# A two-layer graph attention kernel: the first layer's row gathers wait for other matmuls, one wait for each of a pair

## The chip, the cores and the metric

The kernel runs on one core of one Trainium2 chip. A time is the device time of one execution in microseconds. The engines are TensorE (PE in the profile, PEld for its weight loads), VectorE (DVE), ScalarE (ACT), GpSimd (POOL) and SyncE (SP); POOL also issues the indirect transfers (gathers) with which this text deals.

## The reference

Eight graphs of 2048 nodes share one 0/1 adjacency matrix; every node has 64 features. A first attention layer has four heads, a second one has one. Both take the scores from the same projected features on both sides, mask them by the adjacency matrix (with the diagonal set), apply a softmax over the neighbours and average the neighbours' features.

```python
def _gat_layer(h, mask, b):
    scores = jnp.einsum('...nd,...md->...nm', h, h)
    scores = jnp.where(mask, scores, NEG)
    attn = jax.nn.softmax(scores, axis=-1)
    return jnp.einsum('...nm,...md->...nd', attn, h) + b

mask = graph + jnp.eye(N, dtype=graph.dtype) > 0
h = jnp.einsum('bnc,hdc->bhnd', x, Wh)
out_h = _gat_layer(h, mask[None, None], bh[None, :, None, :])
cat = jnp.transpose(out_h, (0, 2, 1, 3)).reshape(B, N, H * D)
z = jax.nn.leaky_relu(cat, negative_slope=0.2)
h2 = jnp.einsum('bnk,dk->bnd', z, Wo)
out2 = _gat_layer(h2, mask[None], bo)
z2 = jax.nn.leaky_relu(out2, negative_slope=0.2)
# layer norm of z2, times gamma, plus beta; then the layer norm of x + that
```

The matrix is sparse: the inputs draw an edge with a probability that falls with the node numbers, 0.4% on the average, and the first nodes have far more neighbours than the rest.

## The kernel before

The first 56 nodes ("hubs") are attended against all 2048 nodes. The other 1992 nodes are cut into 166 sets of 12 (`NS`, `SET`). For each set, VectorE picks the 128 nodes that are neighbours of any of its members and writes their numbers into one column of `index`. The kernel then never forms the full attention matrix: for each set it gathers the 128 rows of features of those nodes from a table in device memory, and attends the 12 members against them under a mask.

A row holds all eight batches, 4 x 130 float32 numbers or 2,080 bytes, so one gather brings 128 rows or 266 KB into one buffer of the pool `rowp`, which has 10 buffers. One gather is one `indirect_dma_start` on POOL's queue (function `gather`, L790 to L793).

The program is written out by hand: every engine runs its instructions in the order in which the program names them, and a framework adds the semaphore waits that the data and the reuse of buffers require. There are three stages: hubs, picks and adjacency loads (to about 150 us in the profile), the first layer's loop (to about 600 us), the second layer.

The first layer's loop (L1017 to L1083) handles two sets at a time, a group; there are 83 groups (`NG`), and step `i` works on several of them at once, each at another stage of its life:

- `scores(i + 1)` (L814): 64 small matmuls; VectorE adds the mask (`weigh`, L826), ScalarE exponentiates (`lift`, L833).
- `project(i - 1)` (L525, matmuls at L531): the head outputs of the group before go through the head weights; ScalarE adds the bias (`leaky`, L518).
- `values(i)` (L837, 32 matmuls at L846): the weighted sums of the gathered rows. It is the last reader of the two row buffers of group `i`. VectorE divides by the sums (`invert`, L848 to L854).
- the gathers of group `i + LOOK`, `LOOK` being 5: both are named right after `values(i)`, and reuse the two buffers that it has just read.
- `own_rows` every second step (POOL, L800), `add_beta` every second step of a later part (POOL, L928), one adjacency load with its conversion in the first nine steps (`more(1)`, POOL at L680 and L687), `keep_own` (POOL, L886), all on POOL's queue in this order.
- `second_maps`, `second_rows`, `columns` (L880, L890, L806): the later life of earlier groups, and the query side of a later one.
- `turn` of the first set of group `i + 3` (L512), `turn_values(i)` (L863, four transposes of the divided sums), `turn` of the second set of group `i + 3` (L512). `turn` is the first reader of a gathered buffer.

So a group gathered in step g - 5 is first read by `turn` near the end of step g - 3, and last by `values` in step g. Ahead of the loop, three groups are gathered; steps -2 and -1 gather groups 3 and 4 into the remaining four of the ten buffers.

The gather before:

```python
def gather(table, s, layer, new):
    t = rows[layer, s] = new(f"g{layer}_{s}")
    nc.gpsimd.indirect_dma_start(out=t.rearrange("n q c -> n (q c)"), out_offset=None, in_=table,
                                 in_offset=bass.IndirectOffsetOnAxis(ap=index[:, s:s + 1], axis=0))
```

Of the kernel before, what the change touches and what calls it, by code (L numbers as in the profile page):

```python
# [359 lines left out]
def fast_kernel(ctx: ExitStack, tc: tile.TileContext, x, adj, Wh, bh, Wo, bo, gamma, beta, out, flag):  # L360


    nc = tc.nc
    B, N, C = x.shape
    H, D, _ = Wh.shape
# [9 lines left out]
    NG = NS // 2  # L375
    M = SET * H
    GM = 2 * Q * SET
# [21 lines left out]
    def half(k):  # L399
        return slice(k * 64, (k + 1) * 64)  # L400
# [10 lines left out]
    ident = const.tile([P, P], F32, name="ident")  # L411
# [4 lines left out]
    whT = early.tile([P, H * D], F32, name="whT")  # L416
# [8 lines left out]
    table1 = dram.tile([N, ROW], F32, name="table1")  # L425
# [9 lines left out]
    index = const.tile([P, NS], I32, name="index")  # L435
# [78 lines left out]
    def leaky(cat, n, name):  # L514

        z = work.tile([P, HP, 2, n], F32, tag="z", name=name, bufs=3)
        for hp in range(HP):
            nc.scalar.activation(z[:, hp], cat[:, :, hp * n:(hp + 1) * n], AF.Identity, bias=bhp[:, hp:hp + 1], scale=1.0)  # L518
        return z

    def leak(z):
        f = z.rearrange("p q s n -> p (q s n)")
        nc.vector.scalar_tensor_tensor(f, f, SLOPE, f, OP.mult, OP.max)

    def project(ot, cat, n):  # L525

        for hp in range(HP):
            for s in range(2):
                for j in range(2):
                    h = 2 * hp + j  # L530
                    nc.tensor.matmul(cat[half(j), s, hp * n:(hp + 1) * n], whT[half(s), h * D:(h + 1) * D],  # L531
                                     ot[half(s), h, :], start=True, stop=True)


    hubm = early.tile([HUB, N], BF16, tag="a", name="hubm", bufs=5)
# [86 lines left out]
    def hub_later(t, new):  # L622

        n = 2 * HUB
        osb = hub_osb[t]

        def turn_back():
            pt = new(f"oth{t}", "T")
            for v in range(2):
                for k in range(2):  # L630
                    nc.tensor.transpose(pt[:, 0, (2 * v + k) * P:(2 * v + k + 1) * P], osb[:, v, k, :], ident)
            ot = held["oth", t] = work.tile([P, H, n], F32, tag="ot", name=f"otbh{t}")
            nc.scalar.copy(ot.rearrange("c h (w n) -> c h w n", w=8),
                           pt[:, 0, :].rearrange("c (w n) -> c w n", w=8)[:, :, :HV].rearrange("c w (n h) -> c h w n", h=H))

        def through_heads():
            cat = new(f"cath{t}", "C")
            project(held.pop(("oth", t)), cat, n)
            z = held["zh", t] = leaky(cat, n, f"zh{t}")
            leak(z)  # L640

        def to_table():
            z = held.pop(("zh", t))
            ph = new(f"hh{t}", "S")
            for p in range(2):
                for hp in range(HP):

                    v = z[:, hp, p, :].rearrange("d (v k m) -> d k v m", v=2, k=2)
                    nc.tensor.matmul(ph[half(p), 0, :n], woT[:, hp, :], v, start=(hp == 0), stop=(hp == HP - 1))
            nc.vector.tensor_copy(ownh[:, t, :], ph[:, 0, :n])  # L650
            nc.tensor.transpose(ph[:n, 1, :P], ownh[:, t, :], ident)
            r = rowts[t]
            nc.vector.tensor_tensor(r[:n, 1:1 + P], ph[:n, 1, :P], bob[:n].rearrange("n p d -> n (p d)"), OP.add)
            dst = table2[:HUB, :].rearrange("n (q c) -> q n c", q=Q)
            for k in range(2):
                nc.sync.dma_start(out=dst[2 * t + k], in_=r[k * HUB:(k + 1) * HUB])

        return [turn_back, through_heads, to_table]
# [128 lines left out]
    rows = {}  # L787
    held = {}

    def gather(table, s, layer, new):  # L790
        t = rows[layer, s] = new(f"g{layer}_{s}")
        nc.gpsimd.indirect_dma_start(out=t.rearrange("n q c -> n (q c)"), out_offset=None, in_=table,  # L792
                                     in_offset=bass.IndirectOffsetOnAxis(ap=index[:, s:s + 1], axis=0))  # L793

    def own_rows(m):

# [17 lines left out]
    def scores(g, sp):  # L814
        xt = held.pop(("T", 1, g)).rearrange("c j (q n) -> c j q n", q=Q)
        y = held["y", g // 2][:, g % 2 * GM:(g % 2 + 1) * GM, :].rearrange("p n h -> p (n h)")
        for j in range(2):
            for q in range(Q):
                for p in range(2):
                    for r in range(2):  # L820
                        nc.tensor.matmul(sp[half(r), p, (q * 2 + j) * M:(q * 2 + j + 1) * M], xt[half(p), j, q, half(r)],  # L821
                                         y[half(p), (j * Q + q) * M:(j * Q + q + 1) * M], start=True, stop=True)
# [33 lines left out]
    def turned(op):  # L856
        return op.rearrange("a j (k c) -> a (j k) c", k=2)[:, :, 2 * (D + 2):2 * (D + 2) + 112]

    def turn_values(g, op):

        osb = held.pop(("o", g))
        for w in range(4):
            nc.tensor.transpose(turned(op)[:, w, :], osb[:112, w].rearrange("a s c -> a (s c)"), ident[:112, :112])  # L863

    def keep_values(g, op):

# [85 lines left out]
    def turns():  # L952
        return bool(picks) and getattr(picks[0], "turns", False)
# [35 lines left out]
    hub_values(*pend)  # L989
    while picks:  # L990
        picks.pop(0)()
    LOOK = 5
    for g in range(LOOK - 2):
        for j in range(2):
            gather(table1, 2 * g + j, 1, rows_tile)
    own_rows(0)
# [10 lines left out]
    def one(name, tag):  # L1007
        return psum1.tile([P, 2, 512], F32, tag=tag, name=name)
# [5 lines left out]
    ready, done = FIRST, 2 * FIRST  # L1014
    todo3 = [(10, 0), (14, 1)]
    slow = hub_later(0, one) + hub_later(1, one)
    for i in range(-4, NG + 3):  # L1017
        if 0 <= i + 1 < NG:
            sp = one(f"s{i + 1}", "S")
            scores(i + 1, sp)  # L1020
            weigh(i + 1, sp)
        if i >= 1 and slow and len(slow) % 3:
            slow.pop(0)()
        cat = one(f"cat{i}", "C")
        if 0 <= i - 1 < NG:
            project(held.pop(("ot", i - 1)), cat, GM)
            held["z", i - 1] = leaky(cat, GM, f"z{i - 1}")
        if 0 <= i + 2 < NG:
            t = held["T", 1, i + 2] = work.tile([P, 2, 512], F32, tag="xTg", name=f"xTg{i + 2}", bufs=3)
            nc.scalar.copy(t, held.pop(("tp", i + 2)))  # L1030
        if 0 <= i + 1 < NG:
            lift(i + 1)
        if 0 <= i < NG:
            op = one(f"o{i}", "O")
            values(i, op)
            invert(i, op)
        if 0 <= i + LOOK < NG and i > -3:
            for j in range(2):
                gather(table1, 2 * (i + LOOK) + j, 1, rows_tile)
        if i + 6 < NG and i % 2 == 0 and i >= -2:  # L1040
            own_rows((i + 6) // 2)
        if 0 <= (i - 30) // 2 <= NV:
            (add_beta if i % 2 else load_own)((i - 30) // 2)
        if 0 <= i - 1 < NG:
            leak(held["z", i - 1])
        if i >= 0:
            if turns():
                some(1)
            if slow and len(slow) % 3 == 0:
                slow.pop(0)()  # L1050
            more(1)
            if todo3 and i == todo3[0][0]:
                make_keys(2, todo3.pop(0)[1], late_two)
            if not picks:
                ready = done
            if not picks and not todo3 and done < NS:
                picks = pick(2)
                done = NS
            assert i + 1 + LOOK >= NG or 2 * (i + 1 + LOOK) + 1 < ready

        if 0 <= i - 2 < NG:
            second_maps(i - 2, cat[:, 0, 384:384 + GM])
        if 0 <= i - 3 < NG:
            second_rows(i - 3, cat[:GM, 1, 384:512])
        if 0 <= i + 4 < NG + NG % 2:
            columns(i + 4, cat)
        if 0 <= i - 2 < NG:
            keep_own(i - 2, cat[:, 0, 384:384 + GM])
        if 0 <= i - 3 < NG:
            keep_rows(i - 3, cat[:GM, 1, 384:512])  # L1070
        for _ in range((2 if i < 22 or i % 2 else 1) if i >= 0 else 0):
            if not turns():
                some(1)
        if 0 <= i + 4 < NG + NG % 2:
            keep_columns(i + 4, cat)
        if 0 <= i + 3 < NG:
            tp = held["tp", i + 3] = one(f"t{i + 3}", "T")
            turn(tp[:, 0, :], rows[1, 2 * (i + 3)])
        if 0 <= i < NG:
            turn_values(i, op)  # L1080
            keep_values(i, op)
        if 0 <= i + 3 < NG:
            turn(tp[:, 1, :], rows[1, 2 * (i + 3) + 1])  # L1083
# [267 lines left out]
    for u in range(-4, NU + 7):  # L1351
        if 0 <= u + 2 < NU:
            scores2(u + 2)
        if 0 <= u < NU:
            a = u % 2
            if a == 0:
                op = bank2(f"o2_{u}", "O")
# [18 lines left out]
        if 0 <= u + 1 < NU:  # L1376
            turn_scores(u + 1)
            a = (u + 1) % 2
# [55 lines left out]
```

## Time and profile before

| What | Value |
|---|---|
| time, median of 3 runs | 1042.88 us (1037.15 to 1049.1) |
| the profiled execution: own time | 880.76 us |
| its span, first to last instruction | 878.9 us |
| mean granted TensorE clock in it | 0.951 |
| TensorE busy (matmuls) | 753.0 us, 86% of the span |
| VectorE, ScalarE, GpSimd busy | 610.1, 514.4, 469.2 us |
| gathers (both layers) | 332, in all 334.9 us busy on POOL, 1009 ns mean |
| gathers' bytes | 88.55 of 145.22 MB moved |

A line of the list of groups or of the timeline gives the source line, the engine, the operation, and the tiles as written<-read, with the count. Times in brackets are an engine's idle time before the instruction and what ended it. The busy time of a gather on POOL is that of its issue; the landing of its data shows only in semaphore events and in what waits for them. The profiled execution was shorter than the timed ones by 162 us; the page shows the profiled one alone.

### The profile page before, as it was taken

How to read it: one execution, taken by the hardware profiler on the slowest of the kernel's cores; microseconds unless marked ns; L12 is line 12 of the kernel's file. 1: busy time of each engine (PE TensorE's matmuls, PEld its weight loads, DVE VectorE, ACT ScalarE, POOL GpSimd, SP SyncE). 2: the span in 40 equal slices, each digit the busy share in tenths (PEclk: the TensorE clock that was granted, in tenths of full speed). 3: DMA queues.
4: the chain of work that ended last, by engine and by line, in shares of the span. 5: the costliest groups of instructions: out<-in, count | busy, mean ns of one | idle time of the engine just before them, and what ended most of it. 6: DMA issues, size and time to landing. Idle time of an engine off the chain costs nothing.

```text
span 878.9 us, 42066 instructions
## 1 busy us (share of the span) xinstructions
PE 753.0 (86%) x18437; PEld 661.2 (75%) x18437; DVE 610.1 (69%) x1369; ACT 514.4 (59%) x961; POOL 469.2 (53%) x612
## 2 busy tenths in 40 slices
PE   1896777889999999999999999992999999998730
PEld 1664456778788999988999999971899999988720
DVE  3356983568888788877555555553258999998994
ACT  2342333556556667666766667651678888886821
POOL 5654141457444555655666666503777777777300
PEclk9998998999999999999999999995999999999965
DMA  8787451355434445655566665514888888888611
GB/s 167 238 218 213 129 146 48 83 142 160 109 100 118 112 125 159 162 169 153 160 168 173 160 166 162 134 28 114 246 266 253 275 275 267 266 252 242 172 46 35
DMA packets 81794, 145.22 MB, mean 165 GB/s; under 512 B 30146, under 2 KB 46466, under 8 KB 81602
## 3 DMA queue, kind: packets, MB, share of 16 engines
q0 software_dynamic: 26720, 88.55, 36.4%
q1 hardware_dynamic: 37842, 49.65, 18.7%
q10 hardware_dynamic: 17040, 4.25, 2.6%
q8 instruction: 147, 2.41, 1.1%
q14 instruction: 45, 0.37, 0.1%
HBM read 123.91 MB, written 18.48 MB: 162 GB/s over the span
## 4 chain that ended last, share of the span: by engine, by line
PE 63%; DVE 15%; DMA 7%; ACT 5%; issue 4%; SPq 3%; POOL 2%; DVEq 0%; ACTq 0%; POOLq 0%
PE t L512 11%; PE s L821 10%; PE o L846 10%; PE cat L806 6%; PE o L863 4%; PE cat L531 4%; PE cat L880 3%; PE s L1133 3%; PE o L1165 3%; PE cat L890 2%; DMA raw<-in_adj_dram 2%; SPq L1248 2%; PE sh L1277 2%; PE e L1144 2%; DMA g<-table,index 1%
## 5 line engine op out<-in xcount | busy, mean ns | idle before, releaser
L792 POOL DMA_INDIRECT g<-table,index x332 | 334.9, 1009 | 236.1 <-PE o L846 140.2
L512 PE MATMUL t<-ident,g 128*128 128x128 f32 x1328 | 182.3, 276 | 15.6 <-DMA g<-table,index 12.7
L512 PEld LDWEIGHTS t<-ident,g 128*128 128x128 f32 x1328 | 154.8, 142 | 20.0 <-issue 14.0
L826 DVE TENSOR_TENSOR e<-s,mask 128x768 f32<-128x768 f32 x83 | 79.4, 956 | 87.4 <-PE s L821 85.4
L518 ACT ACTIVATE z<-cat,bhp 128x192 f32<-128x192 f32 x166 | 60.8, 418 | 85.0 <-PE cat L531 85.0
L846 PE MATMUL o<-g,e 128*64 128x65 f32 x2656 | 97.5, 227 | 0.0
L821 PEld LDWEIGHTS s<-y,xTg 64*64 64x64 f32 x5312 | 85.2, 134 | 13.9 <-issue 13.7
L821 PE MATMUL s<-y,xTg 64*64 64x48 f32 x5312 | 95.5, 220 | 0.0
L846 PEld LDWEIGHTS o<-g,e 128*64 128x64 f32 x2656 | 85.8, 140 | 9.8
L1320 ACT COPY xTg<-t 128x1024 f32<-128x1024 f32 x83 | 80.3, 1017 | 18.1 <-PE t L512 17.3
L1030 ACT COPY xTg<-t 128x1024 f32<-128x1024 f32 x83 | 84.0, 1012 | 2.0 <-PE t L512 2.0
L833 ACT ACTIVATE e<-e,shifts 128x768 f32<-128x768 f32 x83 | 79.2, 955 | 2.1 <-DVE e L826 1.7
L812 ACT COPY y<-cat 128x384 f32<-128x384 f32 (+1 forms) x80 | 40.7, 508 | 64.0 <-PE o L863 40.1
L597 ACT ACTIVATE e<-e,shifts 128x896 f32<-128x896 f32 x32 | 33.4, 1042 | 73.0 <-DVE e L594 52.1
L680 POOL TENSOR_SCALAR a<-raw 120x1024 bf16<-120x1024 int32 (+1 forms) x34 | 38.2, 1125 | 65.1 <-DMA raw<-in_adj_dram 38.4
L806 PE MATMUL cat<-xo,gram 128*128 128x192 f32 (+1 forms) x320 | 65.6, 328 | 0.0
L853 DVE RECIPROCAL rall<-o 64x8 f32<-64x8 f32 x166 | 34.0, 205 | 42.0 <-PE o L846 40.7
L854 DVE TENSOR_TENSOR osb<-o,rall 128x512 f32<-128x512 f32 x83 | 57.4, 692 | 2.9
L1165 PE MATMUL o<-g,es 128*32 128x65 f32 x2656 | 49.1, 226 | 5.9 <-DVE y_s L1188 4.5
L806 PEld LDWEIGHTS cat<-xo,gram 128*128 128x128 f32 x320 | 53.7, 203 | 0.3 <-issue 0.2
L1165 PEld LDWEIGHTS o<-g,es 128*32 128x32 f32 x2656 | 46.1, 113 | 7.0 <-issue 4.9
L1133 PE MATMUL s<-xTg,bd 128*32 128x128 f32 x1328 | 45.4, 277 | 6.2 <-ACT bd L1124 3.5
(177 smaller groups left out, 1369.3 us busy)
## 6 DMA issues: line engine op xcount, KB each, us to landing
raw<-in_adj_dram SPq DMA_DIRECT2D x32, 480.0 KB
table<-xb SPq DMA_DIRECT2D x22, 256.0 KB
xr_s<-table SPq DMA_DIRECT2D x21, 256.0 KB
g<-table,index POOLq DMA_INDIRECT x332
table<-x SPq DMA_DIRECT2D x16, 260.0 KB
x<-in_x_dram ACTq DMA_DIRECT2D x32, 128.0 KB
table<-rowt SPq DMA_DIRECT2D x166, 24.4 KB
xb<-in_x_dram SPq DMA_DIRECT2D x164, 24.0 KB
```

The costliest lines, as they stand in the source:

```text
L512: nc.tensor.transpose(tp[:, q * P:(q + 1) * P], rows[:, q, 1:1 + P], ident)
L518: nc.scalar.activation(z[:, hp], cat[:, :, hp * n:(hp + 1) * n], AF.Identity, bias=bhp[:, hp:hp + 1], scale=1.0)
L792: nc.gpsimd.indirect_dma_start(out=t.rearrange("n q c -> n (q c)"), out_offset=None, in_=table, in_offset=bass.IndirectOffsetOnAxis(ap=ind ...
L806: nc.tensor.matmul(cat[:, k, 2 * GM:2 * GM + n], gram[:, g % 2 * 2 + k, :], held["x", g // 2][:, :n], start=True, stop=True)
L821: nc.tensor.matmul(sp[half(r), p, (q * 2 + j) * M:(q * 2 + j + 1) * M], xt[half(p), j, q, half(r)], y[half(p), (j * Q + q) * M:(j * Q + q ...
L826: nc.vector.tensor_tensor(e[:, :16 * M].rearrange("p (a q n) -> p a q n", a=2, q=Q), sp[:, :, :8 * M].rearrange("p a (q n) -> p a q n", q= ...
L833: nc.scalar.activation(e[:, :16 * M], e[:, :16 * M], AF.Exp, bias=shifts[:, 0:1], scale=1.0)
L846: nc.tensor.matmul(op[half(p), j, o0:o0 + K1], e[:, c0:c0 + 64], rw[j][:, q, sums(p)], start=True, stop=True)
L1030: nc.scalar.copy(t, held.pop(("tp", i + 2)))
L1133: nc.tensor.matmul(sp[q * 32:(q + 1) * 32, k, :], bd[u % 3][:, k, q, :], xt[:, s % 2, q, :], start=True, stop=True, tile_position=(0, q * 32))
L1165: nc.tensor.matmul(op[t * 32:(t + 1) * 32, f, k * W2 + p:k * W2 + p + K1], e[:, 2 * q + p, k, :], rw[:, q, sums(p)], start=(a == 0 and k = ...
L1320: nc.scalar.copy(t, tp)
```

## The change

A gather may now be given an instruction that it has to wait for, besides what its buffer requires. `project` and `turn_values` return their last matmul, and the loop hands these on. The first set's gather of a group is named at the very beginning of a step and waits for the turned values of the step before; the second one is named where both were named, and waits for the projection of its own step. The distance falls from five groups to four; steps -2 and -1 gather groups 3 and 4 as before, step 0 gathers none, and from step 1 on step `i` gathers group `i + 4`.

```diff
@@ project
-                    nc.tensor.matmul(cat[half(j), s, hp * n:(hp + 1) * n], whT[half(s), h * D:(h + 1) * D],
-                                     ot[half(s), h, :], start=True, stop=True)
+                    at = nc.tensor.matmul(cat[half(j), s, hp * n:(hp + 1) * n], whT[half(s), h * D:(h + 1) * D],
+                                          ot[half(s), h, :], start=True, stop=True)
+        return at
@@ gather
-    def gather(table, s, layer, new):
+    def gather(table, s, layer, new, behind=None):
         t = rows[layer, s] = new(f"g{layer}_{s}")
-        nc.gpsimd.indirect_dma_start(out=t.rearrange("n q c -> n (q c)"), out_offset=None, in_=table,
-                                     in_offset=bass.IndirectOffsetOnAxis(ap=index[:, s:s + 1], axis=0))
+        g = nc.gpsimd.indirect_dma_start(out=t.rearrange("n q c -> n (q c)"), out_offset=None, in_=table,
+                                         in_offset=bass.IndirectOffsetOnAxis(ap=index[:, s:s + 1], axis=0))
+        if behind is not None:
+            tc.add_manual_dep(g.ins, behind.ins.name, mybir.DependencyInfo(mybir.DependencyClass.Sync, mybir.DependencyReason.DATA),
+                              reason="the gather's turn")
@@ turn_values
         for w in range(4):
-            nc.tensor.transpose(turned(op)[:, w, :], osb[:112, w].rearrange("a s c -> a (s c)"), ident[:112, :112])
+            at = nc.tensor.transpose(turned(op)[:, w, :], osb[:112, w].rearrange("a s c -> a (s c)"), ident[:112, :112])
+        return at
@@ ahead of the loop
-    LOOK = 5
-    for g in range(LOOK - 2):
+    LOOK = 4
+    for g in range(3):
@@ the loop
+    turned_at = projected_at = None
     for i in range(-4, NG + 3):
+        coming = i + LOOK if i > 0 else i + LOOK + 1 if -2 <= i < 0 else NG
+        if coming < NG:
+            gather(table1, 2 * coming, 1, rows_tile, turned_at)
...
-            project(held.pop(("ot", i - 1)), cat, GM)
+            projected_at = project(held.pop(("ot", i - 1)), cat, GM)
...
-        if 0 <= i + LOOK < NG and i > -3:
-            for j in range(2):
-                gather(table1, 2 * (i + LOOK) + j, 1, rows_tile)
+        if coming < NG:
+            gather(table1, 2 * coming + 1, 1, rows_tile, projected_at)
...
-            turn_values(i, op)
+            turned_at = turn_values(i, op)
```

## The prediction

> **What bounds the kernel now.** I first read the busy shares and the windows, to find which engine sets the length of the first layer's loop.
>
> ```profile
> span 878.9 us, 42066 instructions
> PE 753.0 (86%) x18437; PEld 661.2 (75%) x18437; DVE 610.1 (69%) x1369; ACT 514.4 (59%) x961; POOL 469.2 (53%) x612
> ...
> 400.00:500.00 100.00, 99.62 (x2718) 90.90 (x2711) 60.42 (x145) 67.39 (x138) 61.93 (x80) 1.00 0.60 164
> 225.00:590.00 365.00, 357.90 (x9742) 324.76 (x9742) 255.87 (x655) 241.17 (x497) 197.76 (x262) 1.00 0.52 140
> ```
>
> The columns of the last two lines are stretch, length, and busy time of PE, PEld, DVE, ACT and POOL, then the granted clock, DMA share and GB/s. From 400 to 500 us TensorE is busy for 99.62 of 100 us at full clock, from 225 to 590 us for 357.9 of 365: it sets the step. The list of waits must then say whether any of its few pauses is for a gather.
>
> ```profile
> PE t L512 <- DMA g<-table,index: 12.7, 4, 10.7
> POOL g L792 <- PE o L846: 127.6, 70, 5.2
> POOL a L680 <- DMA raw<-in_adj_dram: 5.4, 2, 2.9
> ```
>
> The first line is of the whole run. All four of its waits lie in the second layer's start near 611 us; TensorE's waits from 150 to 590 us hold none for a gather. The other two, of 180 to 590 us, say who releases the gathers today: the 32 matmuls of `values` (L846), because the buffer to be filled is the one that they have just read. Now one step on the timeline, POOL first (start, length, instruction, and in brackets the idle time before it), then TensorE.
>
> ```profile
> 402.22 0.98 POOL L792 DMA_INDIRECT g<-table,index  x1 [0.88 <-PE o L846]
> 403.51 0.96 POOL L792 DMA_INDIRECT g<-table,index  x1 [0.30 <-PE cat L806]
> 404.47 0.66 POOL L800 COPY xo<-xT 128x192 f32<-128x192 f32 x1
> 405.10 0.25 POOL L886 COPY own<-own 128x96 f32<-128x96 f32 x1
> 408.03 0.97 POOL L792 DMA_INDIRECT g<-table,index  x1 [2.68 <-PE o L846]
> ```
>
> ```profile
> 404.06 0.60 PE L863 MATMUL o<-ident,osb 112*128 112x112 f32 x4 [0.34 <-DVE osb L854]
> ...
> 406.22 0.56 PE L531 MATMUL cat<-otb,whT 64*64 64x96 f32 x16
> ...
> 413.93 0.60 PE L512 MATMUL t<-ident,g 128*128 128x128 f32 x4
> ...
> 414.75 0.60 PE L512 MATMUL t<-ident,g 128*128 128x128 f32 x4
> ```
>
> The reader should see a step of about 5.0 us (402.22 to 408.03 held one pause; 413.93 to 418.9 is the usual gap between turns), the two new releasers (turned values at 404.06, projection at 406.22), and the turns at 413.93 and 414.75 that read the two gathers issued at 402.22 and 403.51.
>
> **What the Trainium skill says.** "DMA: Bandwidth & Descriptors", section "Anatomy of one DMA — SWDGE (gpsimd) path", prices such a DMA at about 2.0 us plus bytes over 436 GB/s; one gather is 128 rows of 2,080 B, 266 KB, so an estimate of 2.6 us. The trace agrees: from the semaphore events, the last count of a gather of the first layer arrives 2.3 us at least, 2.75 us in the median after its issue instruction ends, 4.5 us at most from the fortieth gather on, and up to 7.1 us while adjacency loads run beside it. "Perfetto Trace Analysis", section "DMA Instruction — SWDGE (GPSIMD)", says that the profile's interval of such an instruction ends with the descriptors, not with the data; the same numbers show it (0.97 us against 2.75 more). "TensorE: Matmul & The Clock Gate" lists, in its opening table, GpSimd's queue as strict first-in first-out; below, a gather is seen to stand behind a conversion that waits for its load. The same page, Part 1, says that TensorE idle for some 3.4 us falls to half clock; here the granted clock is 0.70 in the gap from 590 to 630 us.
>
> **The change part by part.**
> *Removed:* the release by `values` and one group of distance. A gather for group g used to be issued in step g-5 behind `values`; now the first is issued behind the turned values of step g-5, the second behind the projection in step g-4. No matmul, copy or DMA is added, and the order on TensorE, VectorE, ScalarE and SyncE is the same; on POOL the pair moves past the own-rows copy, the beta addition, the adjacency conversion and the own copy of one step. Instructions: 332 gathers x 0.97 us before and after, nothing saved.
>
> *Steady steps.* For the group turned at 413.93 and 414.75: the first gather may go at 404.66 by its wait, but the own copy stands before it on POOL until 405.35, so 405.4 + 0.97 + 2.75 = 409.1, 4.8 us early (today 402.22 + 0.98 + 2.75 = 405.95, 8.0 early). The second: projection done at 406.78, issue to 407.9, landed at 410.6, 4.1 early (today 7.5). So about 3.2 us of distance is given away and 4 us is left: nothing on the path. What hides the wait is TensorE's own step; without that cover each late microsecond would be paid every second step, since the turn of group g delays the releases of group g+2. The new waits hold only POOL behind them: the own-rows copy (used two steps later), the beta addition, the conversion, the own copy. All these sit *earlier* after the change, as both releases come before `values`. Replaying POOL's new order with each gather's own landing time, the median spare falls from 7.1 to 4.2 us and the worst after group 14 is 1.6 us, so still nothing.
>
> *Early steps.* Here adjacency loads are still running:
>
> ```profile
> 189.36 1.00 POOL L792 DMA_INDIRECT g<-table,index  x1 [5.19 <-PE o L846]
> ...
> 194.83 1.15 POOL L680 TENSOR_SCALAR a<-raw 120x1024 bf16<-120x1024 int32 x1 [2.50 <-DMA raw<-in_adj_dram]
> ...
> 206.87 1.13 POOL L680 TENSOR_SCALAR a<-raw 120x1024 bf16<-120x1024 int32 x1 [2.95 <-DMA raw<-in_adj_dram]
> ```
>
> Today group 9 is gathered at 189.36, ahead of the conversion that waits for its load. Afterwards it stands behind it: POOL is free at 197.1, issue 197.6 to 198.6, landing 4.8 later as this gather had it, 203.4; its turn is at 201.92: 1.5 us late. The next conversions do the same to groups 10 and 11: the second of 10 is late by 0.5, the two of 11 by 1.5 and 0.4, on top of the slip before. Sum 3.9 us. Bounds: 0, if TensorE had to stand for VectorE's picks there anyway (it is busy 23.87 of 25 us from 200 to 225, so hardly); 4.9, with one microsecond more per landing. I take 3.9. A gain below zero is excluded in the steady part beyond TensorE's idle time: 390 us from 200 to 590 less 381.8 busy leaves 8 us, 0.8% at the very most.
>
> *Sum.* The profiled execution took 880.76 us (span 878.9 and 1.9 around it); plus 3.9 gives 884.7, +0.4%. The median of the timed runs is 1042.88, 162 us or 18% above the profiled one, and nothing in the page says where that lies. Were TensorE's 753 us to run at a clock of 0.78 in place of 0.951, it would be explained (753 x 0.951/0.78 = 918, an estimate); then steps are longer and the spare larger (replayed at steps 1.2 times as long: 2.6 us lost). On the timed runs: 1042.9 + 4 = 1047.
>
> **The rivals.**
> *A, slower:* the unexplained 162 us is late gathers. Place: the turns (L512) of steady steps. It decides from a landing of about 7 us after the issue's end (2.75 + the 4 spare); with 4.5 us more than in the profile, the second gathers (spare 3.8 in the median of the replay) are 0.7 late each and, paid every second step, 78/2 x 0.7 = 27, with the early 4 it is 31: 1074. If gathers bind the kernel before as well, the whole given-away distance, 39 x 2.9 = 113 us, is the end of that road. For it: the gap, and that the loop's DMA share is 0.52 to 0.6. Against: the profile shows no landing that long in steady steps.
> *B, faster:* issuing at the step's edge keeps descriptor writing away from VectorE's reciprocal and product (L853, L854), which TensorE's turn of values awaits, or spreads the two transfers. Against: gathers take 942 ns at least and 974 in the median, so nothing holds them up, and TensorE waits 1.7 us in all for L854. Only something outside the profile could pay; a tenth of the 162 us gives 1027.
> *C, no effect:* the early slip is absorbed and the release order is not binding: 1043.
>
> **How the numbers follow.** Forecast (early slip alone, 1043 to 1052) 0.36, C 0.16, A 0.34, B 0.14. About 1% is what a measurement of this kernel can tell from no change. Forecast and C lie within 1% but for noise (0.46 of 0.52, the rest going to slower); A is slower save for its mildest end (0.02), so slower 0.38, same 0.48, faster 0.14. The range reaches from half-way into B (1030) to a little past A's value (1080); B's better half and A's far end are left out.
>
> **What would show it.** In the profile after: POOL's gathers released by L863 and L531 (their shifted lines) in place of L846; no TensorE wait for a gather from 225 to 590 us; one to four such waits from 198 to 220 us summing to about 4 us; the window 400 to 500 still over 99% busy. I am wrong if the turns wait for gathers throughout (A), or if the timed runs fall by more than 10 us without the profile's steps becoming shorter (B).

## The result, and the profile after

The changed kernel takes 1128.23 us (median of 4, 1125.46 to 1137.13); the kernel before, measured beside it, 1044.79. The ratio is 1.082 [1.073, 1.091]: 83 us slower. The prediction said 1047, with a range to 1080.

The runs fall into two groups by the chip that they ran on: on some chips ("A" below, three of the later sets of runs) the kernel before takes some 880 us, on others ("B", two sets) some 1040. What makes a chip A or B is not known. The profile of before that stands above has the time of A, while the timed runs, and the profile after, have that of B. So the profile after is set against another profile of the kernel before, taken on B in a later run (span 1043.4 us).

The busy shares, the score matmuls' group and the window from 400 to 500 us of after (the group's columns are busy time and mean ns, then the idle time before it and what ended most of that; the window's are those of the prediction):

```profile
span 1127.5 us, 42067 instructions
PE 872.9 (77%) x18437; PEld 711.7 (63%) x18437; DVE 610.6 (54%) x1369; ACT 514.0 (46%) x961; POOL 460.3 (41%) x612
...
L825 PE MATMUL s<-y,xTg 64*64 64x48 f32 x5312 | 134.6, 223 | 32.6 <-issue 29.9
...
400.00:500.00 100.00, 89.01 (x2112) 74.96 (x2112) 57.65 (x157) 52.26 (x108) 47.62 (x62) 1.00 0.46 128
```

The kernel before on B, the same window:

```profile
400.00:500.00 100.00, 97.25 (x2497) 87.05 (x2497) 58.20 (x142) 63.34 (x127) 57.38 (x75) 1.00 0.55 152
```

At full granted clock (1.00) TensorE gets through 2112 matmuls in 100 us instead of 2497, and it does not only pause more: 42.1 ns of busy time stand for one matmul against 38.9. The waits say what it doesn't wait for. TensorE's of after from 150 to 800 us:

```profile
PE s L825 <- issue: 29.9, 70, 0.7
PE o L867 <- DVE osb L858: 18.8, 71, 1.5
...
PE t L512 <- DMA g<-table,index: 12.5, 2, 10.5
```

POOL's from 200 to 800 us:

```profile
POOL g L793 <- PE cat L531: 83.0, 57, 2.9
POOL g L793 <- PE t L512: 29.8, 65, 1.2
```

The second gather is released by the projection (L531), as the change says. The first goes after the turned values, but what holds it last is POOL's own copy ahead of it (L891, which waits for VectorE): the gather starts 0.44 us after that copy's end in all steady steps, on A as on B, so the turn (L512) that the list names is only the signal that came last. The only two waits of TensorE for a gather stand at the start of the second layer (one of 10.5 us, as before); not one lies in the first layer's loop. Instead there are 29.9 us of pauses in the middle of the scores (L825) for which the profile shows no releaser at all ("issue"). One step of after shows where they lie (times as start and length):

```profile
416.25 1.15 PE L850 MATMUL o<-g,e 128*64 128x65 f32 x32
...
416.59 0.96 POOL L793 DMA_INDIRECT g<-table,index  x1 [1.45 <-PE cat L531]
...
417.23 0.50 PE L885 MATMUL cat<-z,woT 128*64 128x96 f32 x8
...
418.07 0.42 DVE L857 RECIPROCAL rall<-o 64x8 f32<-64x8 f32 x2 [1.10 <-PE o L850]
...
419.27 0.60 PE L867 MATMUL o<-ident,osb 112*128 112x112 f32 x4 [0.21 <-DVE osb L858]
...
419.92 0.27 POOL L891 COPY own<-own 128x96 f32<-128x96 f32 x1 [1.84 <-DVE own L890]
...
420.25 1.29 PE L825 MATMUL s<-y,xTg 64*64 64x48 f32 x48
...
420.62 0.97 POOL L793 DMA_INDIRECT g<-table,index  x1 [0.43 <-PE t L512]
...
421.95 0.46 PE L825 MATMUL s<-y,xTg 64*64 64x48 f32 x14 [0.41 <-issue]
...
422.25 0.54 PE L531 MATMUL cat<-otb,whT 64*64 64x96 f32 x15
...
422.71 1.15 PE L850 MATMUL o<-g,e 128*64 128x65 f32 x32
```

And one step of before on B:

```profile
421.27 0.95 POOL L792 DMA_INDIRECT g<-table,index  x1 [0.30 <-issue]
...
422.45 1.35 PE L821 MATMUL s<-y,xTg 64*64 64x48 f32 x64
...
423.60 0.56 PE L531 MATMUL cat<-otb,whT 64*64 64x96 f32 x16
424.10 1.15 PE L846 MATMUL o<-g,e 128*64 128x65 f32 x32
...
425.08 0.50 PE L880 MATMUL cat<-z,woT 128*64 128x96 f32 x8
...
425.30 0.42 DVE L853 RECIPROCAL rall<-o 64x8 f32<-64x8 f32 x2 [0.50 <-PE o L846]
...
425.42 0.97 POOL L792 DMA_INDIRECT g<-table,index  x1 [2.42 <-PE o L846]
```

Before, from the first score to the projection it is 423.60 - 422.45 = 1.15 us, and the reciprocal starts 1.20 us after `values` (425.30 - 424.10). After, a gather is issued *on top of* the scores, at 420.62 to 421.59: they take 422.25 - 420.25 = 2.00 us and stand still for a part of it. The other gather is issued on top of `values`, at 416.59 to 417.55: the reciprocal comes 418.07 - 416.25 = 1.82 us after it.

The two delays are not of one kind. The scores' matmuls start late. Those of `values` do not: the block takes 1.15 us in both kernels, and the next one (L885, before L880) starts 0.98 us after it in both. What is late is the semaphore event that tells of the last `values` matmul. It comes 0.64 us after that matmul's recorded end (median; late in 67 of 68 steps), in the step of before 0.02 us. Since the ends of matmuls are modelled in these profiles, it is open whether the work or only its signal was late.

As medians of the steps 20 to 70 (distances between the starts of the blocks, in us):

| | step | scores to projection | projection to `values` | `values` to reciprocal | turn to turned values | the two issues start, after the scores' start |
|---|---|---|---|---|---|---|
| before on A | 5.00 | 0.97 | 0.46 | 1.20 | 0.44 | 2.75 and 4.02 |
| before on B | 5.35 | 1.28 | 0.49 | 1.20 | 0.44 | 3.09 and 4.38 |
| after on B | 6.45 | 1.92 | 0.54 | 1.82 | 0.80 | 0.37 and 2.80 |

From the second row to the third the path on TensorE gains 0.64 at the scores, 0.05 at the projection and 0.36 where the turned values wait for the later reciprocal, 1.05 in all, and the step 1.10. Times 78 changed steps that is 86 us; the first layer's last `values` ends at 708.3 us after and at 623.4 before, 84.9 later, while what follows is as long as before (419 and 420 us). So nearly the whole loss lies at these places; that the issues are its cause is still a theory: **while POOL issues a gather, and shortly after, TensorE's blocks of many small matmuls are slowed or stopped or their end is told late, and its blocks of a few large ones keep their pace.** Before, both issues fell on the columns and turns (L806, L512), where the step shows no loss; the change moved them onto the scores and `values`. The rival is the prediction's: the gathers come later, by a group less of distance, and something waits for them.

### The profile page after: what moved, and what is told of

Same layout as the page of the kernel before. It is cut to its first block, busy times and chain, and to the rows that moved or that the text cites. A ratio compares the mean times of both kernels' runs of the same rounds, so it can differ in the third digit from the quotient of the medians.

```text
span 1127.5 us, 42067 instructions
## 1 busy us (share of the span) xinstructions
PE 872.9 (77%) x18437; PEld 711.7 (63%) x18437; DVE 610.6 (54%) x1369; ACT 514.0 (46%) x961; POOL 460.3 (41%) x612
## 3 DMA queue, kind: packets, MB, share of 16 engines
q0 software_dynamic: 26720, 88.55, 29.5%
## 4 chain that ended last, share of the span: by engine, by line
PE 63%; DVE 16%; issue 10%; ACT 4%; DMA 3%; POOL 1%; SPq 0%; another core or an unknown queue 0%; ACTq 0%; DVEq 0%; POOLq 0%
PE t L512 14%; PE o L850 11%; PE s L825 11%; DVE osb L858 4%; PE s L1141 4%; PE o L867 4%; PE o L1173 3%; PE cat L531 3%; DVE rall L857 3%; PE e L1152 2%; PE sh L1285 2%; ACT xTg L1328 2%; PE oh L1307 1%; PE sh L591 1%; DVE e L595 1%
## 5 line engine op out<-in xcount | busy, mean ns | idle before, releaser
L793 POOL DMA_INDIRECT g<-table,index x332 | 324.2, 976 | 357.6 <-PE o L1173 126.2
L512 PE MATMUL t<-ident,g 128*128 128x128 f32 x1328 | 204.3, 285 | 26.3 <-DMA g<-table,index 12.6
L512 PEld LDWEIGHTS t<-ident,g 128*128 128x128 f32 x1328 | 161.6, 147 | 47.1 <-issue 38.6
L825 PE MATMUL s<-y,xTg 64*64 64x48 f32 x5312 | 134.6, 223 | 32.6 <-issue 29.9
L825 PEld LDWEIGHTS s<-y,xTg 64*64 64x64 f32 x5312 | 107.8, 134 | 63.3 <-issue 62.1
L1160 DVE TENSOR_TENSOR es<-e,linked 128x384 f32<-128x384 f32 (+1 forms) x42 | 23.1, 550 | 138.2 <-PE t L512 109.7
L1141 PE MATMUL s<-xTg,bd 128*32 128x128 f32 x1328 | 62.9, 302 | 29.4 <-issue 19.7
L891 POOL COPY own<-own 128x96 f32<-128x96 f32 x83 | 22.8, 275 | 148.8 <-DVE own L890 148.8
L1141 PEld LDWEIGHTS s<-xTg,bd 128*32 128x32 f32 x1328 | 41.8, 120 | 46.4 <-issue 36.7
L867 PE MATMUL o<-ident,osb 112*128 112x112 f32 x332 | 49.9, 273 | 18.8 <-DVE osb L858 18.8
```

The lines of the kernel that those rows point to most:

```text
L512: nc.tensor.transpose(tp[:, q * P:(q + 1) * P], rows[:, q, 1:1 + P], ident)
L793: g = nc.gpsimd.indirect_dma_start(out=t.rearrange("n q c -> n (q c)"), out_offset=None, in_=table, in_offset=bass.IndirectOffsetOnAxis(ap ...
L867: at = nc.tensor.transpose(turned(op)[:, w, :], osb[:112, w].rearrange("a s c -> a (s c)"), ident[:112, :112])
L1141: nc.tensor.matmul(sp[q * 32:(q + 1) * 32, k, :], bd[u % 3][:, k, q, :], xt[:, s % 2, q, :], start=True, stop=True, tile_position=(0, q * 32))
```

## The experiments

### Distance against place (kind A)

The first set takes the change apart. *Distance alone*: both gathers behind `values` as before, but for one group later, so four groups ahead as in the changed kernel.

```diff
         if coming < NG:
-            gather(table1, 2 * coming, 1, rows_tile, turned_at)
...
-            gather(table1, 2 * coming + 1, 1, rows_tile, projected_at)
+            for j in range(2):
+                gather(table1, 2 * coming + j, 1, rows_tile, values_at)
```

> Both gathers of a group stay where they were, behind the values matmuls, but one group later (for group i+4 in step i, the first waiting for this step's values): only the shorter distance of the change is kept, by one whole step. S: issues fall on the same work as before, so 1043 (1035 to 1052). Theory R (late gathers, the prediction's rival A): the distance is shorter than in the changed kernel, so at least its 1128.

*First release alone*: the changed kernel with its second added wait left out; with four groups of distance the buffer has long been free, so the second gather follows the first at once.

```diff
-            gather(table1, 2 * coming + 1, 1, rows_tile, projected_at)
+            gather(table1, 2 * coming + 1, 1, rows_tile)
```

> The changed kernel without the second wait: the first gather is released by the turned values, the second follows as soon as its buffer and POOL are free. S: both issues now fall on the scores and the projection, 0.65 us each, so about as slow as the changed kernel, 1100 to 1135. R: the second gather comes earlier than in the changed kernel, so faster than it, 1043 to 1090.

*Second release alone*: the first gather of a group in its old place behind `values`, five groups ahead; only the second behind the projection.

```diff
+        if 0 < i and i + 4 < NG:
+            gather(table1, 2 * (i + 4) + 1, 1, rows_tile, projected_at)
+        if 0 <= i + 5 < NG and i > -3:
+            gather(table1, 2 * (i + 5), 1, rows_tile)
```

> The first gather of a group stays behind the values matmuls of step g-5, the second waits for the projection of step g-4 as in the change. S: one stall in a step, on the values matmuls, so about half of the loss, 1075 to 1095. R: the second gather is the later one and binds, so the whole loss, about 1128.

And the kernel before once more:

> The kernel before, once more with a profile. Theory S (issue on TensorE: while POOL writes a gather's descriptors, TensorE stands still for about 0.65 us, and the scores (L821) and values (L846) matmuls cannot hide it): about 1043 us; a first-layer step of 5.0 to 5.4 us, since both issues fall on the columns and turns, and a second layer as long as in the changed kernel (about 420 us from the last values matmul of the first layer to the end, against 287 in the shown profile), with stalls at its gather issues. Theory P (phase of POOL and VectorE: the pair's new place makes the own copy, the beta addition and VectorE's leaky product collide): also 1043, but with no stall of TensorE at a gather's issue. Rival theory C (granted clock): 1043 with a mean clock under 0.85.

Measured beside a before of 881.85 us: distance alone 886.92, ratio 1.004 [1.001, 1.007]; first release alone 932.85, 1.056 [1.051, 1.061]; second release alone 894.34, 1.013 [1.009, 1.018]; before again 884.02. The expected times for this set were numbers of kind B and missed in the absolute; in ratios, distance alone costs next to nothing, while the kernel that moves both issues forward in the step, at the same distance, loses most. TensorE's waits of distance alone from 200 to 600 us:

```profile
PE t L512 <- DMA g<-table,index: 2.6, 4, 0.9
```

Four late gathers, 2.6 us: this is the early slip that the prediction had priced at 3.9, and half of the 5.1 us that this kernel loses. A step of first release alone:

```profile
406.17 1.51 PE L825 MATMUL s<-y,xTg 64*64 64x48 f32 x64
406.18 0.98 POOL L793 DMA_INDIRECT g<-table,index  x1 [0.44 <-PE o L867]
...
407.46 0.96 POOL L793 DMA_INDIRECT g<-table,index  x1 [0.30 <-issue]
...
407.70 0.81 PE L531 MATMUL cat<-otb,whT 64*64 64x96 f32 x16
...
408.44 1.15 PE L850 MATMUL o<-g,e 128*64 128x65 f32 x32
```

The first issue lies on the scores, the second on the projection: in the medians the first take 1.18 us instead of 0.97, and the projection's distance to `values` is 0.87 instead of 0.46. That is 0.62 us of the 0.78 by which the median step grows; times 78 it is some 48 of the 51 us lost. On A the rival of late gathers falls, and the theory of the place stands; on B the changed kernel's loop, without one wait for a gather, says the same.

### The change again, its first half, and POOL busy without a gather (kind B)

> The kernel before, with a profile on the same chip as the three that follow. Theory S (a gather's issue slows TensorE's scores and projection, its values hardly or not, its larger matmuls not at all): on a chip like that of the last runs 882 with a step of 5.0 us; on a chip like that of the first times 1043, a step of 5.0 to 5.4 us and stalls in the second layer.

> The changed kernel on the chip of these runs. S: its first gather is issued on the scores, its second on the values, so if the kernel before takes 882 here, it lands between the two halves measured, 905 to 935, with the scores stretched from 0.93 to some 1.3 us; if the kernel before takes 1043 here, 1128. Theory R (late gathers): the turns wait for gathers by several tens of us in all.

*First moved alone*: the first gather behind the turned values, the second behind `values`.

```diff
-            gather(table1, 2 * coming + 1, 1, rows_tile, projected_at)
+            gather(table1, 2 * coming + 1, 1, rows_tile, values_at)
```

> The first gather of a group is released by the turned values as in the change, the second by the values matmuls of step g-4, so it stays on the columns and turns. S: one issue a step on the scores, the second free: where the kernel before takes 882, 900 to 925 (0.25 to 0.5 us in each of 78 steps); where it takes 1043, 1080 to 1110. R: the second gather is the later one and has less distance than in the change, so at least as slow as the changed kernel.

*Before with memsets*: the kernel before with four fills of a tile of 128 x 128 on POOL, named where the changed kernel has its first gather, and behind the same instruction.

```diff
+        if 0 < i and i + 4 < NG:
+            m = nc.gpsimd.memset(idle, 0.0)
+            for _ in range(3):
+                nc.gpsimd.memset(idle, 0.0)
+            tc.add_manual_dep(m.ins, turned_at.ins.name, ...
```

> The kernel before, with four memsets of a 128x128 tile added on POOL in each step from 1 to 78, released by the turned values, where the change issues its first gather: POOL is as busy there as with a gather's issue (about 1 us), but nothing is transferred. S: it is the issue of a gather that TensorE feels, not work on POOL, so within 1% of the kernel before. Rival P (POOL's occupation at that point delays what stands behind it): a good part of the loss of the change.

Measured beside a before of 1045.88 us: before again 1045.3; the change again 1123.73, 1.076 [1.069, 1.084]; first moved alone 1094.52, 1.047 [1.039, 1.055]; with memsets 1047.84, 1.004 [1.001, 1.006]. In first moved alone the second issue starts 3.72 us after the scores and touches nothing (the reciprocal is back at 1.20 after `values`), the first starts at 0.17 and stretches the scores to 1.78; the step is 5.86, 0.51 over before, times 78 some 40 of the 49 us. So each half of the change has a price of its own: about 49 us for the first issue on the scores, some 30 more when the second falls on `values`. The window of the kernel with memsets from 400 to 500 us:

```profile
400.00:500.00 100.00, 97.15 (x2477) 86.83 (x2472) 59.16 (x145) 63.47 (x128) 71.48 (x145) 1.00 0.55 150
```

POOL is busy for 71.48 us instead of 57.38, TensorE for 97.15 as against 97.25. The fills do not all fall on the scores, as other work of POOL stands before them: of 51 steps (20 to 70) they lie on the scores for over 0.4 us in 21, where the scores take 1.35 us, and not at all in 20, where they take 1.27. So POOL at work beside the scores costs them some 0.08 us at that overlap, and a gather's issue 0.5 to 0.64 us more than before.

### The issue against its transfer, and no gathers at all

*No gathers in the loop*: the changed kernel, where from the sixth group on no gather is made, the first ten buffers are read over and over, the mask is left open and the flag that asks for a general kernel is held at zero, so the attention of those groups is not that of their sets.

```diff
-            gather(table1, 2 * coming, 1, rows_tile, turned_at)
+            gather(table1, 2 * coming, 1, rows_tile, turned_at) if coming < 5 else again(2 * coming)
...
-            gather(table1, 2 * coming + 1, 1, rows_tile, projected_at)
+            gather(table1, 2 * coming + 1, 1, rows_tile, projected_at) if coming < 5 else again(2 * coming + 1)
```

> The changed kernel without the first layer's gathers from group 5 on: the ten row buffers of groups 0 to 4 are used again and again, under an open mask, and the flag that asks for the general kernel is held at zero (156 transfers and the masking of real neighbours are left out; every other instruction stays). Theory S (a gather's issue stops TensorE): the loop's step falls to 5.0 us, so where the kernel before takes 1045, 1015 to 1035; where it takes 882, 870 to 885. Theory P (POOL's order and VectorE): the step stays at 5.4 us or more.

*Quarter gathers*: the changed kernel, where each of those gathers brings 128 rows of a quarter of the length (520 B): as many descriptors, a quarter of the bytes. Its rows, mask and flag are not those of the reference either.

```diff
-        g = nc.gpsimd.indirect_dma_start(out=t.rearrange("n q c -> n (q c)"), out_offset=None, in_=table,
+        g = nc.gpsimd.indirect_dma_start(out=t[:, 0, :] if part else t.rearrange("n q c -> n (q c)"), out_offset=None,
+                                         in_=table.rearrange("n (q c) -> (n q) c", q=Q) if part else table,
```

> The changed kernel with its first-layer gathers from group 5 on a quarter as long: 128 runs of 520 bytes in place of 2,080, into the buffers of groups 0 to 4, with open mask and the flag held at zero as in the run without gathers. S in its form 'the writing of the descriptors stops TensorE': as many descriptors, so as slow as the changed kernel (within 1.5%; 1110 to 1135, or its time on the other kind of chip). S in its form 'the transfer of the data does': a quarter of the bytes, so most of the loss is gone.

*Both behind the projection*: both gathers of a group behind the projection of their step.

```diff
-            gather(table1, 2 * coming, 1, rows_tile, turned_at)
...
+            for j in range(2):
+                gather(table1, 2 * coming + j, 1, rows_tile, projected_at)
```

> Both gathers of a group wait for the projection of step g-4: the first is issued on the values matmuls, the second on the second maps and the columns. S: nothing falls on the scores; on a chip where before takes 882, within 1.5% of it; where it takes 1045, one stall on the values of about 0.6 us a step but no spill of the second gather into the scores (0.24 us a step in the kernel before): 1060 to 1080. R: the same distance as the second gather of the change, so a loss as large as the change's.

*Behind half the values*: both behind the seventeenth of the 32 matmuls of `values`, so that their issue ends earlier, before the scores.

```diff
+                    if (q, j, p) == (2, 0, 0):
+                        at = m
...
+                gather(table1, 2 * coming + j, 1, rows_tile, values_at)
```

> Both gathers of group i+4 wait for the seventeenth of the 32 values matmuls of step i, half a microsecond ahead of where the kernel before releases them. S: the first gather's stall begins when the values end and the second's ends before the scores start, so the spill into the scores is gone: where before takes 1045, 1025 to 1040; where it takes 882, 875 to 890 (the shorter distance cost 0.4% there). R: slower than before by more than 1%.

Measured, kind A, before 881.21 us: no gathers 875.91, 0.994 [0.992, 0.996]; quarter gathers 902.05, 1.023 [1.018, 1.028]; both behind the projection 902.35, 1.027 [1.022, 1.032]; behind half the values 883.53, 1.004 [1.002, 1.005]. As these were on A, the change itself was run on A beside the same kernels, before 879.4 us:

> The changed kernel beside the three that follow, to have its time on the same chip. S: where the kernel before takes 1045, 1124; where it takes 881, 905 to 925 (scores stretched by 0.4 us as in the run with quarter-length gathers, 902, and nothing for the values).

> The changed kernel with quarter-length gathers, as before. S by descriptors: within 1.5% of the changed kernel on the same chip. S by data: at least half of the loss gone.

> The changed kernel without the first-layer gathers from group 5 on, as before. S: its loop takes 5.0 us a step on either kind of chip; where before takes 1045 (5.24 to 5.6 us a step), 1010 to 1025, about 100 us below the changed kernel.

> Both gathers of group i+4 behind the seventeenth values matmul of step i, as before. S: where before takes 1045, the spill into the scores is gone: 1025 to 1040; where it takes 881, 1.0035 of it again. Rival: the first gather's stall reaches into the values instead and nothing is won, 1045 to 1060.

The change 903.0, 1.027 [1.024, 1.030]; quarter gathers 899.92, 1.024 [1.021, 1.027]; no gathers 876.89, 0.996 [0.994, 0.998]; behind half the values 885.07, 1.006 [1.004, 1.009]. The windows from 400 to 500 us, of the change on A, of quarter gathers and of no gathers:

```profile
400.00:500.00 100.00, 97.52 (x2514) 88.04 (x2515) 60.11 (x144) 63.59 (x130) 58.59 (x74) 1.00 0.55 153
```

```profile
400.00:500.00 100.00, 98.20 (x2584) 88.56 (x2584) 58.55 (x137) 62.97 (x132) 58.01 (x75) 1.00 0.29 80
```

```profile
400.00:500.00 100.00, 99.95 (x2740) 91.33 (x2740) 60.27 (x146) 67.94 (x141) 22.53 (x40) 1.00 0.21 59
```

The last column is GB/s: from the change to the quarter gathers the traffic is nearly halved (153 to 80 GB/s), and the time stays within 0.4%; POOL has as many issues (58.59 and 58.01 us busy). So on A the loss goes with the issue, not with the number of bytes that follow it. With no gathers, in the third fence, TensorE is 99.95% busy. The change on A costs 2.7%, a third of what it costs on B: its step is 5.37, the scores 1.17 and the projection's distance 0.60 in place of 0.97 and 0.46, and `values` lose nothing (1.20).

Both behind the projection was expected to cost little on A (within 1.5%), as its issues miss the scores. It lost 2.7%, and by a second mechanism. VectorE's product in `leaky` (L523), in the run of before on A and then in this kernel (count, then min, median and max in ns):

```profile
L523 DVE SCALAR_TENSOR_TENSOR z<-z x56: 546/550/859, 279.7 to 558.2; 128x384 f32<-128x384 f32 x56
```

```profile
L523 DVE SCALAR_TENSOR_TENSOR z<-z x52: 548/674/2082, 283.1 to 554.5; 128x384 f32<-128x384 f32 x52
```

And TensorE's projections of that kernel wait, from 270 to 590 us:

```profile
PE cat L531 <- DVE e L830: 6.3, 6, 1.1
PE cat L531 <- ACT otb L875: 5.3, 6, 1.1
```

The median step stays 5.00, with the first issue on `values`; but from step 32 on, where `add_beta` (POOL, L933, 1.28 us) runs every second step, it can meet that product, which is then held up to 2.08 us, and ten steps more than in before, at first every second one, take about 6.3 us, while ScalarE's copy for the projection (L875) comes late. Ten times 1.25 us is 12.5 of the 15 us that the profiled run lost (896.59 us); the timed runs lose 21 in the median, and the rest was not traced. "SBUF — State Buffer", section "SBUF: two separate sides", describes a loss of this kind: an instruction of VectorE with two SBUF inputs and one of GpSimd that reads SBUF share one pair of ports as an exclusive lock, the one that starts first has it, and the other waits for the whole instruction. The trace agrees in part: between 280 and 560 us all 12 products of over 1 us overlap the addition. But in ten of them the product starts first on record, by 0.2 to 0.4 us and while the gather's issue still runs, and four other products overlap the addition and take 0.55. No run here moved `add_beta` away by itself. Second release alone, above, has the same long steps from the same place on, ten more than in before, or some 12.5 of the 19 us that its profiled run lost (901.28), so its 1.3% are not evidence for the main mechanism.

### On kind B again

> As before. S: where before takes 1045, 1025 to 1040; the rival (the first gather's stall reaches into the values): 1045 to 1060. Where before takes 881: 1.003 to 1.008 of it again.

> As before. S: the loop takes 5.0 us a step on either kind of chip; where before takes 1045, 1010 to 1025.

Measured, before 1037.83 us: behind half the values 1047.7, 1.010 [1.006, 1.013]; no gathers 1008.28, 0.969 [0.965, 0.974], a little under the expected range. A step without gathers:

```profile
419.25 1.15 PE L831 MATMUL s<-y,xTg 64*64 64x48 f32 x64
...
420.22 0.53 PE L531 MATMUL cat<-otb,whT 64*64 64x96 f32 x16
...
420.68 1.15 PE L856 MATMUL o<-g,e 128*64 128x65 f32 x32
```

Scores 0.97 and projection 0.46: exactly those of A, and the step is 5.00 as there. So what the kernel before loses on B in this loop (5.35 against 5.00; 78 x 0.35 = 27 of the 29.5 us that this run gained) goes with its gathers as well. In before its second issue ends as the scores start (4.38 + 0.96 of 5.35), so what stretches them comes after the issue. Moving both issues earlier was to win these 27 us, and did not: behind half the values the issues are over 0.3 us before the scores, which still take 1.31, and the run is 1% slower. What slows TensorE there stays open. The gathers' data is under way by then (it starts some 0.7 us after an issue's end), and quarter gathers did not run on B, so there the transfer is a rival that no run excludes. No version tried beats the kernel before.

### The pause itself

In the trace of after, all but one of the some 100 pauses of 0.2 to 1.2 us inside the scores (steps 20 to 70, from one matmul's start to the next) overlap the issue of a gather, and so in the changed kernel's second run on B. The issue covers half of the scores there, so by chance well over half would overlap it. There are often two in one issue: they begin 0.3 to 0.7 us after it begins (tenth to ninetieth percentile), and the later ones end some 0.37 us after it ends. The gather's first packet of data comes some 0.33 us later still, so its data is not what stops TensorE in these pauses. In before on B it is otherwise: the scores have 28 such pauses in those steps, none overlaps an issue, and they begin some 0.35 us after the second issue's end and are over 0.5 to 0.8 us after it, while the data of the pair's first gather is under way. On A full stops are few: 18 in the changed kernel, of about 0.3 us, against none in before; in most steps the spacing of the score matmuls goes from 14.5 ns to 25 to 47 ns between 0.6 and 1.0 us after the issue begins. A late fetch of TensorE's own program is not a likely cause. "Runtime: NRT & Kernel Launch", section "Instruction fetch mechanics", says that a program is refilled in blocks of 16 KiB, and the trace has such packets, 147 of 16,384 bytes; but in the second run on B one comes about every 6 us from 250 to 590 us, and only some 26 of 100 pauses of the scores meet one, not far from what chance gives (a packet of 1.0 us and a pause of 0.47, 1.5 of 6.1 us, 24%).

What is not shown is *what* in the issue holds TensorE. Two readings are that the writing of the transfer's descriptors gets in the way of TensorE's reads, or that something keeps TensorE's instructions from starting. "SBUF — State Buffer", in the section named above, says that TensorE never waits for anyone inside that memory. If that holds, the second reading is left; the runs can't tell them apart. That blocks of large matmuls keep their pace fits both. The late event behind `values`, with all starts around it on time, is explained by neither as it stands.

## Why the prediction was wrong

- *The bound.* Right: TensorE set the step, at 99.6% before on A, and the loss is a loss on TensorE.
- *Removed: "332 gathers x 0.97 us before and after, nothing saved".* This is the step that failed. The count and the price are right (POOL's busy time hardly changes), but the issue was priced on POOL alone. The same 0.97 us cost the step nothing on columns and turns of before on A; on B they cost 0.64 us more than in before on the scores, and on `values` they let VectorE's reciprocal start 0.62 us later, of which 0.36 reaches the path. The prediction asked of each issue when its data lands, and not what TensorE does while it is issued. The timeline that it shows has the answer half in view: both issues stood, in all steady steps, on large matmuls. As no steady step of before has a gather on the scores, the price could not be read there, only bounded, and the bound taken was zero.
- *Steady steps: 4 us of spare, "nothing on the path".* Right as to the data: no gather is late in the steady steps, and distance alone costs 0.4% on A. Wrong as to the path, through the issues.
- *Early steps: 3.9 us.* Measured 2.6 in distance alone and 2.8 in the changed kernel on A. On B it is gone; longer steps give the gathers more time there, which may be why.
- *The 162 us between the profiled and the timed runs.* Tried as a lower clock, 0.78 as an estimate. It is the other kind of chip. Span by span, the first layer's last `values` end at 595.2 of 882.1 us on A and at 623.4 of 1043.4 on B: 28 us come from there and 133 from the second layer. The mean granted clock is 0.928 there, not 0.78. Why the second layer is so much longer on B was not tried. It gathers all along, and in its middle the recorded semaphore events of TensorE come more than 0.15 us after the matmul's end 150 times of 322 on B and 12 of 319 on A, which points the same way and shows no cause.
- *Rival A, slower by late gathers, 1074.* The sign was right and the cause wrong: landing was not the term. *Rival B, faster through gathers away from VectorE's reciprocal:* it looked at the right place with the wrong sign: the change moved an issue onto `values`, and with it that reciprocal is late by 0.62 us. *C, no effect:* not on either kind (2.7% on A, 8% on B).
- *What would show it.* "POOL's gathers released by L863 and L531": the second so; the first goes behind POOL's own copy, as the prediction's steady steps had said. "No TensorE wait for a gather from 225 to 590 us": so. "One to four such waits from 198 to 220 us": none on B, two on A. "The window 400 to 500 still over 99% busy": it is 89.01, with no wait for a gather in it; the prediction had no case for that. "Wrong if the turns wait for gathers throughout": they don't, and the prediction was wrong all the same.

## What to carry to other kernels

Where TensorE bounds a loop, the place of a gather's issue within the step can be a cost of its own: look at which matmuls it falls on, and try first to let it fall on a few large ones rather than on many small ones. Before the data's landing time is worked out to the microsecond, ask what the issue does to the other engines while it lasts, and where the profile has no instance of that overlap, leave room for it on the slow side. And if timed runs and a profiled one differ by a sixth, compare stage by stage before explaining it by a clock.

## What was not expected of the hardware

- The issue of one gather (128 rows, 0.97 us on POOL), against the kernel before: 64 small matmuls (64 x 64 by 48) take 0.64 us more on B and 0.20 on A; 16 matmuls of the projection 0.41 us more on A; behind 32 matmuls of 128 x 64 by 65 VectorE starts 0.62 us later on B and no later on A, though the matmuls' starts are unchanged; the large matmuls (128 x 128 by 128 or 192) start at their usual pace on both. On A a quarter of the bytes doesn't make it cheaper; on B fills on POOL near its place cost 0.4% of the time.
- The same program takes about 880 us on one kind of chip and 1040 on the other; without gathers in the first layer's loop, the steps of that loop are equal on both, 5.00 us.
- A product on VectorE (L523, both inputs the same tile) that met a two-input addition on POOL (L933) beside a gather's issue went from 0.55 to 2.08 us, and about ten steps grew from 5.0 to 6.3 us.
